# Attention maxima one pair ahead and in bfloat16 parts, a chunk's last sum in the next chunk, squares laid out token by token

## The chip, the cores and the metric

The kernel runs on one core of a Trainium2 chip. The metric is the device time of one execution in microseconds (us). A core has five engines that each work through their own queue: TensorE (PE, matrix products; its weight loads are listed apart as PEld), VectorE (DVE), ScalarE (ACT), GpSimd (POOL), and SyncE (SP), which issues the transfers. Matrix products go into PSUM, which is used here in banks of 512 floats per partition; all else lies in SBUF.

## The reference

Two blocks of a network act on x of 16 sequences, 512 tokens and 256 channels. Each block has an attention part and a feed-forward part; both are normalised, scaled, shifted and gated per sequence.

The attention of block 0 is a recurrence over chunks of 16 tokens, for every sequence and each of 16 heads, with two small weight matrices (4 x 16) that change from chunk to chunk:

```python
def step(carry, xs):
    W_in, W_out = carry
    q_t, k_t, v_t, lr_t = xs
    k_h = softmax(einsum('blhd,bDhd->blhD', k_t, W_in)) * lr_t[..., 1:]
    q_h = softmax(einsum('blhd,bDhd->blhD', q_t, W_in))
    qk = einsum('bqhD,bkhD->bhqk', q_h, k_h) * mask
    o_t = einsum('bqhD,bDhd->bqhd', q_h, W_out) + einsum('bhqk,bkhd->bqhd', qk, v_t)
    W_out = W_out + einsum('bnhD,bnhd->bDhd', k_h, v_t)
    for _ in range(2):
        g_out = -attn(W_in, k_t, v_t)
        g_in = -attn(W_out, v_t, k_t)
        W_in = W_in - lr_in * g_in
        W_out = W_out - lr_out * g_out
    return ((W_in, W_out), o_t)
```

Before it, q and k are divided by their length over the 16 channels of a head, and after it o is normalised over the same channels; both need a sum of squares per token. The feed-forward of block 0 is `gelu(x U1 V1 + b1) U2 V2 + b2`. Block 1 has a softmax attention in which a token sees the 64 last tokens and tokens 0 to 3, and a feed-forward `sigmoid(xr W_r) * (relu(xk W_k)^2 W_v)`.

## The kernel before, in words

**Units.** A unit is 8 sequences (a half) by 64 tokens; there are 16. Each passes through five streams: `prepare` (projections, short convolutions), `chain` (the recurrence), `mlp` (end of block 0's attention, then `low_rank_ffn`), `attend` (`window_attention`), `mix` (`channel_mix`). `timetable` gives every step of a stream a due time; the steps are emitted in that order, two chains (one of each half) always side by side and in the same phase. The framework's scheduler then orders the instructions of each engine by these priorities and its own estimate of when they are ready; on the chip each queue runs in the order so built, and tiles come from rings of buffers.

**The recurrence** (`recur`, one call per chunk, seven steps). Every product of tokens and weights is one elementwise instruction of 1024 numbers per partition and a reduction: `scores` multiplies on DVE (L500) and reduces on DVE (L501); `outer` multiplies on POOL (L507, tiles pd_o, pd_kv, pd_i) and `total` reduces on DVE (L603, tiles do, di). A softmax over tokens is `exp_tokens` (maximum, difference, the exponential on ACT, L515) and `over_tokens` (L520 to L522). In the order of a chunk: scores of k and q; their softmaxes; outer products pd_o (its sum do1, L608) and pd_kv; a running sum over the tokens (L598); scores of v; pd_i twice; scores of k again; pd_o again; and as the last sum of the chunk `do2`, which gives W_out (L624). All product tiles share one ring of five buffers (`prod`), for both halves. Two chunks are a piece of 32 tokens; `load_piece` loads k, v and q and divides by the lengths, `finish_piece` normalises o.

**Squares.** ACT writes the squares in the order of the tile, channel by channel, and `sum_d` (L529) reduces them on DVE over the channels, which lie 32 numbers apart.

**The attention** (`window_attention`). It goes by pairs of sequences r = 0 to 3. For a pair: scores sc, query by key, into four banks (`abank`, a ring of four that st, py, pz and the ph of `low_rank_ffn` share), with the mask added by a bfloat16 product (L828); their maxima over keys on DVE (L850), for all but the first two token blocks also over the four global keys (sg, mg, L862); the maxima turned by PE (L865) and copied by ACT (L867) to mxT; then the same scores key by query, st, from which the maxima are subtracted by products of a selector and mxT; the exponential on ACT (L883); the products with the values and with ones (py, pz); the reciprocal by a logarithm and an exponential (L932, L933); yT on DVE (L937); the projection. The float32 selectors `sel` and `selg` are columns of a constant called parity. The helper `mm` stands for nearly all products there, so they have one line, L831.

**The bias b2** is added in `low_rank_ffn` as a product of a row of ones and the row b2, once for each sequence pair (L724).

Where a function of ACT needs another table, ACT loads it (ACT_TABLE_LOAD); `run` keeps the instructions of a burst of one table together (L204) and loads the usual table again after it (L214).

Of the kernel before, what the change touches and what calls it, by code (L numbers as in the profile page):

```python
# [10 lines left out]
F32 = mybir.dt.float32  # L11
# [20 lines left out]
NS = 4  # L32
F, RANK = 1024, 64
# [34 lines left out]
def parity_scales():  # L68

    ch = np.arange(P)
    even = (ch // D) % 2 == 0
    s = 1.0 / math.sqrt(D)
    group, slot = ch // 32, ch % 32
    sel = -(slot[:, None] == np.arange(NS)[None, :]).astype(np.float32)
    k2, pair, _ = np.unravel_index(np.arange(32), (2, 4, NGLOB))
    selg = np.stack(
        [(group[:, None] == pair) & (slot[:, None] == 2 * k2 + e) for e in range(2)], 1  # L80
    ).astype(np.float32)
    ones_g = np.tile(np.arange(8)[None, :] == (4 * k2 + pair)[:, None], (NR, 1))
    parts = [
        np.stack([even * s, ~even * s, even, ~even], 1),
        group[:, None] == np.arange(4)[None, :],
        sel,
        -selg.reshape(P, -1),
        ones_g,
    ]
    return np.ascontiguousarray(np.concatenate([p.astype(np.float32) for p in parts], 1))  # L90
# [3 lines left out]
def adaln_blocks(ctx: ExitStack, tc: tile.TileContext, a: dict, out: bass.AP):  # L94
# [71 lines left out]
    b2_row = ctile([1, C], "b2_row")  # L166
    nc.sync.dma_start(b2_row, a["V2b"][RANK:])
# [8 lines left out]
    parity, rowgrp, sel = marks[:, :4], marks[:, 4:8], marks[:, 8 : 8 + NS]  # L176
    selg = marks[:, 8 + NS : 72 + NS].rearrange("p (n k) -> p n k", n=2)
    ones_g = marks[:, 72 + NS :]
    ones = ctile([P, 32], "ones")
    nc.vector.memset(ones, 1.0)  # L180
    masks = const.tile([P, 12, P], BF16, tag="masks", name="masks")
# [12 lines left out]
    def log_sigmoid_tail(src, tmp):  # L194
# [3 lines left out]
        nc.scalar.activation(tmp, tmp, AF.Ln, bias=1.0)  # L198

# [26 lines left out]
    with tc.tile_pool(name="mod", bufs=1) as mp:  # L226
        masks_f = mp.tile([P, 12, P], F32, tag="masks_f", name="masks_f")
        nc.sync.dma_start(masks_f, a["masks"].rearrange("p (n k) -> p n k", n=12))
        nc.vector.tensor_copy(masks, masks_f)
        wp = mp.tile([P, 2, C], F32, tag="wp", name="wp")  # L230
# [59 lines left out]
    maxima = [ctile([P, P], f"maxima{n}") for n in range(2)]  # L290
# [237 lines left out]
    def sum_d(t, x, tag):  # L528
        nc.vector.tensor_reduce(t, x.rearrange("p d t -> p t d"), AX.X, add)  # L529

    def load_piece(u, pc):
# [14 lines left out]
        for n in "kq":  # L546
            sq = big(half, f"sq_{n}{tag}")[:, : D * PT].rearrange("p (d t) -> p d t", d=D)
            nc.scalar.activation(sq, s[n], AF.Square)
            ss = small(half, f"ss_{n}{tag}", PT)
            sum_d(ss, sq, tag)  # L550
            inverse_root(ss)
            nc.gpsimd.tensor_tensor(s[n], s[n], over_d(ss), mul)
        return s

    def recur(u, pc, c, s):
# [15 lines left out]
        scores(half, nc.vector, q, w_in, sc[:, :, CH:], f"q{tag}")  # L571
        p_out = exp_tokens(half, sc[:, :, :CH], R, f["mx_k"], f"k{tag}")
# [51 lines left out]
        nc.vector.tensor_tensor(w_out, total(d_out, "do2"), w_outs[:, R:], add)  # L624
# [7 lines left out]
    def finish_piece(u, pc, s):  # L632
# [7 lines left out]
        sum_d(mean, o, tag)  # L640
        nc.scalar.activation(mean, mean, AF.Copy, scale=1.0 / D)
        nc.gpsimd.tensor_tensor(o, o, over_d(mean), sub)
        sq = big(half, f"osq{tag}")[:, : D * PT].rearrange("p (d t) -> p d t", d=D)
        nc.scalar.activation(sq, o, AF.Square)
        var = small(half, f"ov{tag}", PT)
        sum_d(var, sq, tag)
# [39 lines left out]
    def low_rank_ffn(i, x):  # L686
# [27 lines left out]
        yield  # L714
        qT = t2k("b", f"QT{i}")
        nc.scalar.copy(qT, pq)
        for b2 in range(2):
            gt = load_gate("b", 1, b0 + 4 * b2, f"b{i}_{b2}")
            po = bank(f"pv2{i}_{b2}")
            for n in range(2):  # L720
                r = 2 * b2 + n
                dst = po[:, n * C : (n + 1) * C]
                nc.tensor.matmul(dst, lhsT=qT[:, r * P : (r + 1) * P], rhs=w_v2, start=True, stop=False)
                nc.tensor.matmul(dst, lhsT=ones[:1, :1].to_broadcast([1, P]), rhs=b2_row, start=False, stop=True)  # L724
# [3 lines left out]
    def window_attention(i, x):  # L728
# [105 lines left out]
        for b2 in range(NR // 2):  # L834
            gt = load_gate("c", 2, b0 + 4 * b2, f"c{i}_{b2}")
            outs = []
            for n in range(2):
                r = 2 * b2 + n
                tag = f"{i}_{r}"
                q = lambda k2, e: qs[:, k2, 2 * r + e].rearrange("p h t -> p (h t)")  # L840

                sc = [abank(f"sc{tag}_{j}") for j in range(4)]
                for s, k2, e in slots:
                    for j in range(4):
                        rows = slice(32 * j, 32 * (j + 1))
                        mm(sc[j][:, s * P : (s + 1) * P], q(k2, e)[rows], window(r, k2, e)[rows], s == 0)
                mx = maxima[r % 2]
                for j in range(4):
                    add_mask(sc[j], True)
                    nc.vector.tensor_reduce(  # L850
                        mx[:, 32 * j : 32 * j + NS], sc[j].rearrange("p (s k) -> p s k", s=NS), AX.X, ALU.max
                    )
                if far:
                    sg = bank(f"sg{tag}")
                    for s, k2, e in slots:
                        mm(sg[:, 16 * s : 16 * (s + 1)], q(k2, e), kglob[:, b0 + 2 * r + e, 32 * k2 : 32 * k2 + 16], s == 0)
                    mg = work.tile([P, 16], F32, tag="mg", name=f"mg{tag}", bufs=2)
                    nc.vector.tensor_reduce(
                        mg, sg[:, :64].rearrange("p (x g) -> p x g", g=NGLOB), AX.X, ALU.max
                    )  # L860
                    mv = mx.rearrange("p (j x) -> p j x", j=4)[:, :, :NS]
                    nc.vector.tensor_tensor(mv, mv, mg.rearrange("p (s j) -> p j s", s=NS), ALU.max)  # L862
                yield
                pt = bank(f"pmx{tag}")
                nc.tensor.transpose(pt[:, :P], mx, ident)  # L865
                mxT = work.tile([P, P], F32, tag="mxT", name=f"mxT{tag}", bufs=1)
                nc.scalar.copy(mxT, pt[:, :P])  # L867

                st = [abank(f"st{tag}_{j}") for j in range(4)]
                for s, k2, e in slots:  # L870
                    for j in range(4):
                        rows = slice(32 * j, 32 * (j + 1))
                        mm(st[j][:, s * P : (s + 1) * P], window(r, k2, e)[rows], q(k2, e)[rows], s == 0)
                for s, k2, e in slots:
                    for j in range(4):
                        rows = slice(32 * j, 32 * (j + 1))
                        mm(st[j][:, s * P : (s + 1) * P], sel[rows, s : s + 1].to_broadcast([32, P]), mxT[rows])
                yield
                pT = []
                for j in range(4):  # L880
                    add_mask(st[j], False)
                    pT.append(t2k("c", f"pT{tag}_{j}"))
                    nc.scalar.activation(pT[j], st[j], AF.Exp)  # L883
                py, pz = abank(f"py{tag}"), abank(f"pz{tag}")
                if far:

                    rg = slice(32 * r, 32 * (r + 1))
                    tg = bank(f"tg{tag}")
                    for s, k2, e in slots:
                        mm(tg[rg, e * P : (e + 1) * P], kglob[:, b0 + 2 * r + e, 16 * k2 : 16 * k2 + 32], q(k2, e), s == 0)  # L890
                    for e in range(2):
                        mm(tg[rg, e * P : (e + 1) * P], selg[:, e], mxT)
                    pg = work.tile([P, 2 * P], F32, tag="pg", name=f"pg{tag}", bufs=1)
                    nc.scalar.activation(pg[rg], tg[rg, : 2 * P], AF.Exp)
                    for s, k2, e in slots:
                        for j in range(4):
                            cols = slice(k2 * P + 32 * j, k2 * P + 32 * (j + 1))
                            mm(
                                py[32 * j : 32 * (j + 1), s * P : (s + 1) * P],
                                vglob[half][rg, e, cols],  # L900
                                pg[rg, e * P : (e + 1) * P],
                                s == 0,
                            )
                    for k2 in range(2):
                        for j in range(4):
                            n = 4 * k2 + j
                            mm(
                                pz[32 * j : 32 * (j + 1), k2 * 2 * P : (k2 + 1) * 2 * P],
                                ones_g[rg, n : n + 1].to_broadcast([32, 32]),
                                pg[rg],  # L910
                                k2 == 0,
                            )
                for s, k2, e in slots:
                    for j in range(4):
# [3 lines left out]
                            values[:, r, e, cols],  # L918
                            pT[j][:, s * P : (s + 1) * P],
                            s == 0 and not far,  # L920
                        )
                for s, k2, e in slots:
                    for j in range(4):
                        mm(
                            pz[32 * j : 32 * (j + 1), s * P : (s + 1) * P],
                            ones,
                            pT[j][:, s * P : (s + 1) * P],
                            s == 0 and not far,
                        )
                yield  # L930
# [206 lines left out]
```

## Time and profile before

| | us |
|---|---|
| runs without a profile: median of 3 (lowest, highest) | 3312.57 (3311.25, 3323.61) |
| the profiled execution: its own time | 3313.35 |
| its span, first to last instruction | 3311.6 |
| table loads on ACT, all lines: one | 1.28 |
| one outer product on POOL (L507) | 2.35 |
| one product or reduction of the recurrence on DVE (L500, L501, L603) | 1.21 to 1.22 |
| one reduction to maxima (L850) | 0.68 |

The mean granted clock of TensorE was 0.815 of full speed. Names of tiles are given without the numbers of unit, pair and chunk, so that `do` covers both do1 and do2 and one row stands for all units. A row of groups gives line, engine, operation, what is written and read with partitions and elements, the count; then the busy time in us and the mean of one in ns; then how long the engine had been idle before them and what ended most of that. An fp32 product shows as two records. A row of waits gives who waited for whom, the us in total, how often, and the longest. A row of stages gives the stretch and its length, the busy time of each engine, then the granted clock, the share of the transfer engines and GB/s.

### The profile page before, as it was taken

How to read it: one execution, taken by the hardware profiler on the slowest of the kernel's cores; microseconds unless marked ns; L12 is line 12 of the kernel's file. 1: busy time of each engine (PE TensorE's matmuls, PEld its weight loads, DVE VectorE, ACT ScalarE, POOL GpSimd, SP SyncE). 2: the span in 40 equal slices, each digit the busy share in tenths (PEclk: the TensorE clock that was granted, in tenths of full speed). 3: DMA queues.
4: the chain of work that ended last, by engine and by line, in shares of the span. 5: the costliest groups of instructions: out<-in, count | busy, mean ns of one | idle time of the engine just before them, and what ended most of it. 6: DMA issues, size and time to landing. Idle time of an engine off the chain costs nothing.

```text
span 3311.6 us, 48552 instructions
## 1 busy us (share of the span) xinstructions
PE 2415.2 (73%) x18000; PEld 1495.9 (45%) x18000; DVE 2404.3 (73%) x4510; ACT 1714.0 (52%) x3731; POOL 1613.8 (49%) x1255
## 2 busy tenths in 40 slices
PE   3550155868687787878788787877777787889996
PEld 2110124444344454444545445454445555556674
DVE  1678787778878888888787888878787887864211
ACT  1662254556465645565665546565565544454542
POOL 0335555455556555545556554645546565644101
PEclk9765576879788787888888788888888787878988
DMA  5330113131314122230313123140413221122000
GB/s 148 78 67 15 45 31 70 30 72 43 77 33 97 37 68 62 51 79 27 94 29 97 39 57 74 37 94 21 100 23 82 48 58 46 46 49 58 17 27 26
DMA packets 439215, 186.54 MB, mean 56 GB/s; under 512 B 323841, under 2 KB 412994, under 8 KB 438978
## 3 DMA queue, kind: packets, MB, share of 16 engines
q1 hardware_dynamic: 438978, 183.44, 23.0%
q8 instruction: 141, 2.31, 0.3%
q14 instruction: 96, 0.79, 0.1%
HBM read 116.66 MB, written 66.72 MB: 55 GB/s over the span
## 4 chain that ended last, share of the span: by engine, by line
DVE 36%; POOL 23%; PE 19%; ACT 10%; issue 9%; DMA 2%; SPq 1%; POOLq 0%; ACTq 0%; DVEq 0%
POOL pd_i L507 6%; POOL pd_o L507 6%; DVE pd_kv L598 4%; DVE sc_v L500 3%; DVE sv L501 3%; POOL pd_kv L507 3%; DVE pp L433 3%; DVE maxima L850 2%; DVE di L603 2%; PE ph L704 2%; PE st L831 2%; DVE scs L501 2%; DVE do L603 2%; DVE sc_k L500 2%; PE pp L415 2%
## 5 line engine op out<-in xcount | busy, mean ns | idle before, releaser
L507 POOL TENSOR_TENSOR pd_o<-e_k,dt_v 128x1024 f32<-128x1024 f32 x128 | 299.3, 2348 | 331.1 <-DVE e_k L522 330.9
L507 POOL TENSOR_TENSOR pd_i<-e_v,dt_k 128x1024 f32<-128x1024 f32 x128 | 296.5, 2350 | 73.4 <-DVE e_v L522 73.4
L831 PE MATMUL st<-qs,keys 32*128 32x128 f32 x2048 | 244.1, 384 | 118.4 <-DVE maxima L850 116.9
L831 PEld LDWEIGHTS st<-qs,keys 32*128 32x128 f32 x2048 | 206.3, 265 | 164.3 <-DVE maxima L850 138.9
L603 DVE TENSOR_REDUCE do<-pd_o 128x64 f32<-128x1024 f32 x128 | 155.7, 1216 | 158.0 <-POOL pd_o L507 157.8
L628 POOL TENSOR_TENSOR pd_kv<-hid,pd_kv 128x1024 f32<-128x1024 f32 x64 | 150.5, 2352 | 151.9 <-DVE fw L599 148.8
L603 DVE TENSOR_REDUCE di<-pd_i 128x64 f32<-128x1024 f32 x128 | 155.6, 1215 | 94.6 <-POOL pd_i L507 94.6
L676 PE MATMUL pwo<-w_WoT,oT 128*128 128x256 f32 x256 | 103.4, 567 | 148.1 <-POOL oT L669 148.1
L831 PE MATMUL sc<-keys,qs 32*128 32x128 f32 x2048 | 169.1, 307 | 58.1 <-DVE yT L937 33.9
L850 DVE TENSOR_REDUCE maxima<-sc 128x4 f32<-128x512 f32 x256 | 166.6, 680 | 35.7 <-PE sc L828 35.7
L831 PEld LDWEIGHTS sc<-keys,qs 32*128 32x128 f32 x2048 | 136.7, 199 | 114.5 <-issue 41.9
L598 DVE TENSOR_TENSOR_SCAN pd_kv<-within,pd_kv 128x1024 f32<-128x1024 bf16 x64 | 174.4, 2725 | 0.4
L500 DVE TENSOR_TENSOR sc_k<-tok,fw 128x1024 f32<-128x1024 f32 x128 | 155.8, 1217 | 17.5 <-ACT tok L565 15.2
L507 POOL TENSOR_TENSOR pd_kv<-hid,dt_v 128x1024 f32<-128x1024 f32 x64 | 150.4, 2350 | 33.1 <-DVE hid L590 28.9
L883 ACT ACTIVATE pT<-st 128x512 f32<-128x512 f32 x256 | 133.5, 620 | 35.5 <-PE st L828 35.5
L500 DVE TENSOR_TENSOR sc_v<-tok,fw 128x1024 f32<-128x1024 f32 x128 | 150.9, 1212 | 0.9
L501 DVE TENSOR_REDUCE sv<-sc_v 128x64 f32<-128x1024 f32 x128 | 151.0, 1208 | 0.0
L997 POOL TENSOR_TENSOR ka<-ka 128x512 f32<-128x512 f32 x32 | 32.8, 1039 | 238.1 <-ACT ka L996 238.1
L947 PE MATMUL pproj<-w_proj,yT 128*128 128x256 f32 x512 | 131.5, 402 | 23.4 <-DVE yT L937 19.6
L676 PEld LDWEIGHTS pwo<-w_WoT,oT 128*128 128x128 f32 x256 | 70.2, 291 | 172.4 <-POOL oT L669 157.0
L204 ACT ACT_TABLE_LOAD x104 | 133.4, 1283 | 25.8 <-PE ph L704 16.4
L428 ACT COPY xp<-pp 128x512 f32<-128x512 f32 x96 | 56.7, 590 | 170.9 <-PE pp L415 159.3
(237 smaller groups left out, 6823.5 us busy)
## 6 DMA issues: line engine op xcount, KB each, us to landing
values<-values SPq DMA_DIRECT2D x56, 256.0 KB
gate_a<-gates SPq DMA_DIRECT2D x64, 128.0 KB
xa<-in_x_dram SPq DMA_DIRECT2D x32, 256.0 KB
x<-in_x_dram SPq DMA_DIRECT2D x32, 256.0 KB
gate_c<-gates SPq DMA_DIRECT2D x64, 128.0 KB
gate_d<-gates SPq DMA_DIRECT2D x64, 128.0 KB
q<-y SPq DMA_DIRECT2D x64, 128.0 KB
dt_q<-q SPq DMA_DIRECT2D x32, 256.0 KB
```

What stands on the lines that cost most here:

```text
L204: ins = nc.scalar.activation(*args[0], **args[1])
L500: engine.tensor_tensor(pr, tok.unsqueeze(1).to_broadcast(every), w.unsqueeze(2).to_broadcast(every), mul)
L501: nc.vector.tensor_reduce(dst, pr, AX.X, add)
L507: engine.tensor_tensor(pr, hid.unsqueeze(2).to_broadcast(every), tok.unsqueeze(1).to_broadcast(every), mul)
L598: nc.vector.tensor_tensor_scan(flat, within, flat, 0.0, mul, add)
L603: nc.vector.tensor_reduce(t, pr, AX.X, add)
L628: nc.gpsimd.tensor_tensor(po, qh.unsqueeze(2).to_broadcast([P, R, D, CH]), upto, mul)
L676: nc.tensor.matmul(po[:, n * C : (n + 1) * C], lhsT=pair(oT, k, 2 * b2 + n), rhs=w_o[:, k, :], start=k == 0, stop=k == 1,)
L831: nc.tensor.matmul(dst, lhsT=lhsT, rhs=rhs, start=start, stop=False, skip_group_check=True)
L850: nc.vector.tensor_reduce(mx[:, 32 * j : 32 * j + NS], sc[j].rearrange("p (s k) -> p s k", s=NS), AX.X, ALU.max)
L883: nc.scalar.activation(pT[j], st[j], AF.Exp)
L947: nc.tensor.matmul(po[:, n * C : (n + 1) * C], lhsT=yT[:, k2, par].rearrange("p e t -> p (e t)"), rhs=w_proj[:, k2, par, :], start=k2 == 0 ...
```

## The change

It has five parts.

1. The work on a pair is split into `find_maxima` (scores, maxima) and `weigh` (all the rest). The first pair's maxima are found ahead of the loop, and then those of pair r + 1 are issued before pair r is weighed.
2. The maxima are kept as three bfloat16 numbers that add up to the float32 one, in 12 of each 32 columns of the tile `maxima`, made by five small instructions on POOL (`in_parts`). The tile, the identity that turns it, mxT and the selectors are bfloat16; a selector now has a one for each of the three parts.
3. b2 is three bfloat16 rows (`bias2`), made at the start by DVE and moved to three partitions by three small transfers; one product over a whole bank adds it for both pairs, ahead of the products with V2.
4. The last sum of a chunk and its addition to W_out (`do2`) are kept as a function and called in the next chunk of the same half, after the scores of k and q. After the last chunk of a half they are left out, since nothing reads W_out then.
5. ACT writes the squares token by token, so that the 16 that are added lie side by side; `squares` takes the place of `sum_d`.

```diff
-    sel = -(slot[:, None] == np.arange(NS)[None, :]).astype(np.float32)
+    part = slot // NS < NPART
+    sel = -((slot[:, None] % NS == np.arange(NS)[None, :]) & part[:, None]).astype(np.float32)
...
+    sel_bf = const.tile([P, NS + 64], BF16, tag="sel_bf", name="sel_bf")
+    nc.vector.tensor_copy(sel_bf, marks[:, 8 : 72 + NS])
...
+    def in_parts(engine, parts, x, rest):
+
+        for n in range(NPART):
+            engine.tensor_copy(parts[n], x)
+            if n < NPART - 1:
+                engine.tensor_tensor(rest, x, parts[n], sub)
+                x = rest
...
+        in_parts(nc.vector, [b2_parts[:, n] for n in range(NPART)], b2_row, b2_row)
+        for n in range(NPART):
+            nc.sync.dma_start(bias2[n : n + 1], b2_parts[:, n])
...
-    maxima = [ctile([P, P], f"maxima{n}") for n in range(2)]
+    maxima = [const.tile([P, P], BF16, tag=f"maxima{n}", name=f"maxima{n}") for n in range(2)]
...
-    def sum_d(t, x, tag):
-        nc.vector.tensor_reduce(t, x.rearrange("p d t -> p t d"), AX.X, add)
+    def squares(half, x, name):
+
+        sq = big(half, name)[:, : D * PT].rearrange("p (t d) -> p t d", d=D)
+        nc.scalar.activation(sq.rearrange("p t d -> p d t"), x, AF.Square)
+        return sq
...
-            sq = big(half, f"sq_{n}{tag}")[:, : D * PT].rearrange("p (d t) -> p d t", d=D)
-            nc.scalar.activation(sq, s[n], AF.Square)
+            sq = squares(half, s[n], f"sq_{n}{tag}")
             ss = small(half, f"ss_{n}{tag}", PT)
-            sum_d(ss, sq, tag)
+            nc.vector.tensor_reduce(ss, sq, AX.X, add)
...
         scores(half, nc.vector, q, w_in, sc[:, :, CH:], f"q{tag}")
+        late[half]()
         p_out = exp_tokens(half, sc[:, :, :CH], R, f["mx_k"], f"k{tag}")
...
-        nc.vector.tensor_tensor(w_out, total(d_out, "do2"), w_outs[:, R:], add)
+        late[half] = lambda: nc.vector.tensor_tensor(w_out, total(d_out, "do2"), w_outs[:, R:], add)
...
+            nc.tensor.matmul(
+                po, lhsT=ones_bf, rhs=b2_rows, start=True, stop=False, skip_group_check=True
+            )
...
-                nc.tensor.matmul(dst, lhsT=ones[:1, :1].to_broadcast([1, P]), rhs=b2_row, start=False, stop=True)
...
+        def find_maxima(r):
...
+            mx = work.tile([P, 4, NS], F32, tag="mx", name=f"mx{tag}", bufs=2)
+            for j in range(4):
+                add_mask(sc[j], True)
+                nc.vector.tensor_reduce(
+                    mx[:, j], sc[j].rearrange("p (s k) -> p s k", s=NS), AX.X, ALU.max
+                )
...
+            parts = maxima[r % 2].rearrange("p (j x) -> p j x", j=4)
+            rest = work.tile([P, 4, NS], F32, tag="rest", name=f"rest{tag}", bufs=2)
+            in_parts(nc.gpsimd, [parts[:, :, NS * n : NS * (n + 1)] for n in range(NPART)], mx, rest)
+
+        def weigh(r, outs):
...
-                nc.tensor.transpose(pt[:, :P], mx, ident)
-                mxT = work.tile([P, P], F32, tag="mxT", name=f"mxT{tag}", bufs=1)
+            nc.tensor.matmul(pt[:, :P], lhsT=maxima[r % 2], rhs=ident_bf, start=True, stop=True)
+            mxT = work.tile([P, P], BF16, tag="mxT", name=f"mxT{tag}", bufs=1)
...
+        find_maxima(0)
+        yield
+        for b2 in range(NR // 2):
+            gt = load_gate("c", 2, b0 + 4 * b2, f"c{i}_{b2}")
+            outs = []
+            for r in (2 * b2, 2 * b2 + 1):
+                if r + 1 < NR:
+                    find_maxima(r + 1)
+                    yield
+                yield from weigh(r, outs)
+                yield
```

The number of steps of `attend` in the timetable is the same as before.

## The prediction

> **What bounds the kernel now.** I read the page first (busy shares and slices), then the busy times of three stages, then those of one unit, then who waits for whom, last the groups.
>
> ```profile
> span 3311.6 us, 48552 instructions
> PE 2415.2 (73%) x18000; PEld 1495.9 (45%) x18000; DVE 2404.3 (73%) x4510; ACT 1714.0 (52%) x3731; POOL 1613.8 (49%) x1255
> PE   3550155868687787878788787877777787889996
> DVE  1678787778878888888787888878787887864211
> POOL 0335555455556555545556554645546565644101
> ```
>
> There are three stages: a start with little for PE, a long middle in which PE and VectorE (DVE) are about equally busy, and an end with PE alone. The sums by stage (PE, weight loads, DVE, ACT, POOL):
>
> ```profile
> 0.00:522.00 522.00, 201.51 (x476) 90.44 (x476) 352.21 (x643) 213.74 (x453) 217.27 (x197) 0.71 0.29 66
> 522.00:3026.00 2504.00, 1966.92 (x15033) 1232.40 (x15033) 1990.41 (x3722) 1380.66 (x3026) 1351.97 (x1013) 0.83 0.24 58
> 3026.00:3312.00 286.00, 246.74 (x2492) 173.06 (x2491) 61.66 (x145) 119.54 (x254) 44.52 (x47) 0.87 0.11 29
> ...
> sum 188.02, PE 149.68 PEld 93.41 DVE 151.30 ACT 106.33 POOL 100.22; mean PE 74.84 PEld 46.71 DVE 75.65 ACT 53.17 POOL 50.11
> ```
>
> The last line is one unit in the middle (1712.56 to 1900.58): 188 us, DVE 151, PE 150. No engine is full; the time is the busy time of DVE plus the waits that two coupled queues impose. What DVE waits for in the middle:
>
> ```profile
> DVE do L603 <- POOL pd_o L507: 132.5, 85, 3.6
> DVE di L603 <- POOL pd_i L507: 78.7, 50, 3.1
> DVE yT L937 <- ACT rs L933: 29.6, 14, 3.5
> DVE up_a L361 <- PE pwo L676: 19.8, 13, 2.1
> DVE up_c L361 <- PE pproj L947: 14.8, 11, 2.5
> ```
>
> And PE over the whole run, then the groups that the change touches or is priced by:
>
> ```profile
> PE st L831 <- DVE maxima L850: 116.9, 36, 8.0
> ...
> L831 PE MATMUL st<-mxT,c_parity 32*128 32x128 f32 x2048 | 113.7, 358 | 4.8 <-ACT mxT L867 4.8
> L724 PE MATMUL pv<-b_row,ones 1*128 1x256 f32 x128 | 46.6, 445 | 0.0
> L529 DVE TENSOR_REDUCE ss_k<-sq_k 128x32 f32<-128x512 f32 x32 | 32.3, 1010 | 2.0 <-ACT sq_k L548 2.0
> L501 DVE TENSOR_REDUCE sv<-sc_v 128x64 f32<-128x1024 f32 x128 | 151.0, 1208 | 0.0
> L520 DVE TENSOR_REDUCE fw<-e_v 128x8 f32<-128x128 f32 x64 | 18.4, 288 | 3.4 <-ACT e_v L515 1.7
> L430 POOL COPY tails<-xp 128x24 f32<-128x24 f32 x84 | 20.1, 240 | 65.0 <-ACT xp L428 62.9 <-ACT om L641 1.9
> ```
>
> **What the Trainium skill says.** "PSUM — Partial Sum Buffer", section "Engine vs sequencer instructions": the queues of ScalarE, VectorE and GpSimdE are strictly first in, first out. The trace agrees: at 1733.62 a pd_o product on POOL starts only after two ka squares, the first of which waited 15.29 us for ACT. "SBUF — State Buffer", section "Door 1: The DMA port swizzle": SBUF lines are 16 bytes, and an access that crosses into a new line pays. The trace agrees for reads: L529 reads 512 elements with a stride in 1010 ns, L501 1024 adjacent ones in 1208. "FP8 and Floating Point Precision", section "TensorE Precision Notes": true FP32 takes four passes. The trace has four bf16 mask products of 512 columns (L828) in 0.97 us, 0.24 each, and an fp32 one (L704) in two records, 1.1 us. "ScalarE: Activation LUTs", section "What ACT_TABLE_LOAD costs": 1283 ns and a drain of about 1380. The trace shows the 1283, and the activation after it 20 ns later; I use 1.28 us.
>
> **The change part by part.**
>
> *bf16 selectors, maxima and bias (PE).* Per pair of sequences, 16 selector products into st are 32 fp32 records, 113.7 / 64 = 1.78 us; undisturbed, 32 such records take 1.07 us, 33 ns each[...]. In bf16 there are 16 records, about 0.53 us; I take 0.9 saved (0.5 to 1.2). The two selectors of tg and the turned maxima halve: 0.5 together. So 1.4 us a pair, 64 pairs: 90. The bias falls from 128 records, 46.6 us, to 32 bf16 products at 0.26: 38 saved. PE loses about 128 us, 8 a unit. In the end stage PE is the bound: 324 records there read mxT or the selectors, 36 a pair, so 9 pairs x 1.4 = 12.6, and one unit's bias 2.4: **-15**. In the middle it counts only where DVE waits on PE's side: yT, up_a, up_c, together 64 us. With 8 of PE's 150 us gone and mxT ready early I take a third: **-20** (0 to -64).
>
> *Maxima one pair ahead.* This looks as if it removed PE's 117 us wait for the maxima. It does not: four banks hold either scores sc or weights st, so st of a pair now waits until DVE has read sc of the next pair. The chain maxima, turn, copy, selectors goes off PE's path, the bank wait stays. Beyond what is counted above I take 0.
>
> *Parts on POOL.* Five small instructions per pair, 320 in all. Copies of 24 elements take 240 ns; at 0.22 each that is 1.1 us a pair, 70 us, in a POOL that is idle half the time. They stand in line, though: in the order built from the changed program the fourth pair's five are right ahead of pd_o, the third's ahead of pd_i. Two exposed groups a unit for 13 units are 29; I take **+10** (0 to 70).
>
> *The chunk's last sum (do2).* Of the 132.5 us above, sorting the L603 reductions by the addition after them (L608 or L624), 58.6 of the run's waits belong to the second sum. In the new order sc_k, sc_q and their reductions of the next chunk, 4 x 1.2 us, come first, longer than the product of 2.35, so this wait goes. Late next is do1, whose 75 us stay. The pd_o buffer is held longer: the ring has five, at most two are held so, three remain. Where a piece ends the reduction already comes first in the new order. I take 60%: **-35** (0 to -58).
>
> *Squares token by token.* 96 reductions (k, q, o in 32 pieces) become contiguous: between 288 ns for 128 elements and 1208 for 1024, 512 give 0.68 against 1.01 to 1.05. 96 x 0.34 = 33 us of DVE; at DVE's 79% of the middle **-25**. ACT now writes with a stride. No row shows that; the strided read of tok (256 elements, 643 ns against about 420 by the rows of 128 and 512) bounds it: 0 to +0.45 us each, 0 to 43 us on an engine busy 55%. Seven more table loads in the new order (ACT puts e_k inside the gelu burst) are 9 us. For both **+5** (0 to 50).
>
> *Start.* Three small loads of the bias parts wait in SP's queue for DVE, with w_init and the second wm behind them; that wm waits until 38 us anyway for its buffer. 0 (to +4).
>
> Sum: -15 -20 +10 -35 -25 +5 = -80. The profiled execution took 3313.35 (span 3311.6), within 1 us of the median 3312.57: **3233 us**.
>
> **The rivals.** *Waits fill up again.* A wait removed from one of two coupled queues returns at the next: only busy time counts, -25 and -15: 3273. For it: DVE and PE are equally full, do1 and di remain. Against: do2's cover is DVE's own work.
>
> *More falls away.* ka's squares stood ahead of pd_o1 and cost do1 3.6 and 1.4 us a unit; in the new order they stand among the pd_i products. That would be 5 x 13 = 65 more, and the 64 us of PE-side waits wholly 44 more: 3124. Against: ka can then hold up pd_i.
>
> *Slower: the chain stands behind PE.* In the new order the second chunk's e_k is normalised on DVE (L541) only after the fourth pair's maxima and the second up_b. PE's work from the first ph to that up_b's product, by the durations of before (8 ph 8.8, 8 pQ 8, pr 3.7, pproj 3.5, scores and masks 2.9, plr and pp 3.5, pkv 1.9, bias and pv 2.2, small ones 3.5), is 38 us, and it starts some 4.6 before e_k2. With 1.1 on POOL and 2.4 on DVE, pd_o1 starts 37 us after e_k2; before it was 1703.33 to 1733.62, 30.3. Seven us a unit, 12 units, +84, against -40 of sure gains: 3357. It decides from 3.3 us a unit. Against: much of DVE's later work is done in that time.
>
> **How the numbers follow.** Forecast 0.43 (own range 3190 to 3275), refilled waits 0.22, more falls away 0.17, slower 0.18. About 0.5%, 17 us, is what a measurement of this kernel can tell from no change. Faster: 0.43 + 0.21 + 0.17 less a little; same 0.04; slower 0.16. The range takes in the third rival's better half and the slower one's beginning, 3130 to 3335.
>
> **What would show it.** Right: L624's sums without waits; ss, ov near 0.68 us; selector products under 0.6 us a pair; the stage after the last chain some 15 us shorter; the unit at 183 us. Wrong: DVE idle before e_k or the last maxima with PE as releaser; POOL's product waiting on the parts; a unit at or over 188.

## The result, and the profile after

The changed kernel took 3296.14 us (median of 5 runs, 3289.18 to 3303.97) beside 3317.76 for the kernel before in the same session: a ratio of 0.9937 (95% interval 0.9913 to 0.9961). It is 0.6% faster, some 21 us, a quarter of the 80 that the prediction gave. Its profiled execution took 3303.97, 3302.2 of them in the span; the mean granted clock of PE was 0.780 (before 0.815). This execution is the slowest of the five, and the other four had 0.785 to 0.789, so the profile shows less than half of the gain and a clock somewhat lower than usual.

The page after (busy time, share and instructions by engine, then two engines in 40 slices):

```profile
span 3302.2 us, 46348 instructions
PE 2424.1 (73%) x16784; PEld 1461.5 (44%) x16784; DVE 2396.2 (73%) x4513; ACT 1762.1 (53%) x3738; POOL 1669.3 (51%) x1575
...
PE   3541255777787878788887878788797878878886
DVE  1678787868887787788778877877878877774221
```

PE has 1216 records fewer and is busy 9 us *longer*. The same three stages after, columns as before:

```profile
0.00:522.00 522.00, 205.24 (x506) 94.86 (x506) 359.34 (x660) 221.88 (x464) 224.92 (x209) 0.67 0.28 66
522.00:3026.00 2504.00, 1993.54 (x13999) 1215.08 (x14000) 1979.59 (x3719) 1420.53 (x3029) 1392.88 (x1281) 0.80 0.24 58
3026.00:3302.00 276.00, 225.30 (x2285) 151.57 (x2282) 57.27 (x136) 119.71 (x248) 51.46 (x86) 0.85 0.10 28
```

In the middle DVE idles 2504 - 1980 = 524 us; before it was 514. The unit there is hardly shorter (before 188.02):

```profile
sum 187.50, PE 153.01 PEld 92.08 DVE 151.91 ACT 110.27 POOL 102.80; mean PE 76.51 PEld 46.04 DVE 75.95 ACT 55.13 POOL 51.40
```

What DVE waits for in the middle after:

```profile
DVE do L628 <- POOL pd_o L526: 87.4, 54, 4.1
DVE di L628 <- POOL pd_i L526: 68.2, 48, 3.2
DVE yT L972 <- ACT rs L968: 33.9, 16, 4.5
DVE ss_q L571 <- ACT sq_q L550: 25.1, 7, 6.7
DVE mix L1022 <- ACT mix L1021: 22.4, 7, 8.3
DVE ov L670 <- ACT osq L550: 20.2, 19, 3.1
DVE sc_q L519 <- ACT tok L589: 19.6, 24, 3.1
DVE pd_kv L620 <- POOL pd_kv L526: 18.8, 11, 2.5
DVE up_c L380 <- PE pproj L994: 18.6, 15, 9.5
```

The waits for do and di fell from 211.2 to 155.6 us, as meant. Waits for ACT grew by as much in the same stretch: ov from 0.3 to 20.2, qs from 0.5 to 17.7, mix from 10.1 to 22.4, fw (for e_k) from 5.2 to 17.2. What was taken from one producer stands at another.

Now PE, in the groups of after:

```profile
L865 PE MATMUL st<-mxT,sel_bf 32*128 32x128 bf16 x1024 | 55.1, 247 | 29.6 <-ACT mxT L902 29.5
L745 PE MATMUL pv<-bias,ones_bf 3*128 3x512 bf16 x32 | 12.3, 383 | 0.0
L865 PE MATMUL py<-pT,values 128*32 128x128 f32 x2048 | 130.4, 374 | 26.8 <-ACT pT L918 26.3
L865 PE MATMUL py<-pg,vglob 32*32 32x128 f32 x1536 | 71.8, 342 | 99.1 <-ACT pg L929 99.1
L865 PE MATMUL pz<-pg,c_parity 32*32 32x256 f32 x768 | 86.8, 534 | 0.0
```

and two of these groups before:

```profile
L831 PE MATMUL py<-pT,values 128*32 128x128 f32 x2048 | 96.4, 289 | 21.0 <-ACT pT L883 20.6
L831 PE MATMUL pz<-pg,c_parity 32*32 32x256 f32 x768 | 57.2, 378 | 0.0
```

The products that were changed cost what was forecast: st's selectors 113.7 to 55.1, the bias 46.6 to 12.3, with the two small ones 119 us less (forecast 128). But products that nobody touched became longer: py from pT by 34, pz from pg by 30, the other two of that kind (pz from pT, py from pg) by 50, together 113. Why is seen in the granted clock. Four stretches of after's middle, columns as in the stages, the granted clock third from the end, and two more that show how long the clock stayed down:

```profile
1739.00:1743.00 4.00, 3.25 (x48) 2.06 (x46) 2.48 (x7) 3.07 (x6) 3.92 (x6) 1.00 0.21 69
1743.00:1748.50 5.50, 0.00 (x0) 0.00 (x0) 5.01 (x13) 4.47 (x7) 5.42 (x7) 0.77 0.54 145
1748.50:1752.00 3.50, 3.45 (x48) 2.13 (x48) 2.31 (x4) 1.09 (x2) 2.04 (x2) 0.50 0.80 154
1752.00:1756.00 4.00, 4.00 (x70) 3.26 (x67) 3.93 (x3) 0.00 (x0) 1.44 (x1) 0.50 0.83 131
...
1748.50:1756.20 7.70, 7.65 (x115) 5.58 (x116) 6.40 (x7) 1.09 (x2) 3.64 (x3) 0.50 0.80 138
1756.20:1759.61 3.41, 0.85 (x8) 0.50 (x6) 3.41 (x4) 0.00 (x0) 3.33 (x2) 1.00 0.00 0
```

PE idles for 5.5 us, its clock drops from 1.00 to 0.50, and it stays there for the work that follows. PE's timeline at that place (start, length, in brackets the wait) in after:

```profile
1748.55 1.93 PE L865 MATMUL py<-pg,vglob 32*32 32x128 f32 x32 [5.59 <-ACT pg L929]
```

and in before:

```profile
1773.26 1.07 PE L831 MATMUL py<-pg,vglob 32*32 32x128 f32 x32 [1.08 <-ACT pg L894]
```

The same 32 records take 1.93 instead of 1.07 us. The Trainium skill, "TensorE: Matmul & The Clock Gate", section "Part 1: The HAM clock gate (the "warmup" mystery)", states this: half rate after an idle window of some 3.4 us, full rate after a busy one. The trace agrees on the fall: PE fell idle at 1742.96 and the clock fell at 1745.96, 3.0 us later. The rise took longer here: PE was busy for 7.65 of 7.70 us before the clock rose at 1756.20. In both traces the record of the clock has no value but 1.0 and 0.5, so a mean of 0.780 is 44% of the span at half rate and 0.815 is 37%: about 230 us more in this execution. Laid over PE's busy time, half rate covers 807 us of it before and 1030 after. Half of the difference, 112 us, is about what the four groups gained (113), an estimate from the two traces. The prediction has no term for it.

PE's waits over the whole run after, to be held against 116.9 us of st for the maxima before:

```profile
PE py L865 <- ACT pg L929: 99.1, 40, 5.7
PE st L865 <- DVE mx L881: 47.8, 16, 5.8
PE sc L865 <- DVE mx L881: 43.4, 22, 6.8
PE st L865 <- ACT rs L967: 36.1, 6, 6.3
```

The bank wait stays, spread over st and sc: with all releasers of their banks, st and sc waited 118.4 + 58.1 us before and 107.2 + 63.0 after. And py's wait for ACT's exponential over the global keys, 17.8 before, became 99.1.

### The profile page after: what moved, and what is told of

It reads as the page before. It is cut to its first block, busy times and chain, and to the rows that moved or that the text cites. A ratio compares the mean times of both kernels' runs of the same rounds, so it can differ in the third digit from the quotient of the medians.

```text
span 3302.2 us, 46348 instructions
## 1 busy us (share of the span) xinstructions
PE 2424.1 (73%) x16784; PEld 1461.5 (44%) x16784; DVE 2396.2 (73%) x4513; ACT 1762.1 (53%) x3738; POOL 1669.3 (51%) x1575
## 4 chain that ended last, share of the span: by engine, by line
DVE 32%; PE 28%; POOL 18%; ACT 11%; issue 7%; DMA 3%; SPq 1%; POOLq 0%; DVEq 0%; ACTq 0%
POOL pd_o L526 4%; POOL pd_i L526 4%; DVE pd_kv L623 4%; DVE pp L452 3%; DVE sc_v L519 3%; PE ph L728 3%; PE py L865 3%; PE st L865 2%; PE pz L865 2%; DVE sv L520 2%; PE pproj L994 2%; POOL pd_kv L526 2%; DVE mx L881 2%; DVE do L628 2%; PE pka L1031 2%
## 5 line engine op out<-in xcount | busy, mean ns | idle before, releaser
L865 PE MATMUL st<-qs,keys 32*128 32x128 f32 x2048 | 234.3, 351 | 107.2 <-DVE mx L881 47.8
L865 PEld LDWEIGHTS st<-qs,keys 32*128 32x128 f32 x2048 | 199.5, 240 | 163.0 <-DVE mx L881 61.5
L881 DVE TENSOR_REDUCE mx<-sc 128x4 f32<-128x512 f32 x256 | 168.4, 679 | 19.0 <-PE sc L862 19.0
L865 PE MATMUL py<-pT,values 128*32 128x128 f32 x2048 | 130.4, 374 | 26.8 <-ACT pT L918 26.3
L972 DVE TENSOR_TENSOR yT<-py,rs 128x256 f32<-128x256 f32 x128 | 51.5, 415 | 133.8 <-ACT rs L968 133.7
L865 PE MATMUL py<-pg,vglob 32*32 32x128 f32 x1536 | 71.8, 342 | 99.1 <-ACT pg L929 99.1
```

The lines of the kernel that those rows point to most:

```text
L865: nc.tensor.matmul(dst, lhsT=lhsT, rhs=rhs, start=start, stop=False, skip_group_check=True)
L881: nc.vector.tensor_reduce(mx[:, j], sc[j].rearrange("p (s k) -> p s k", s=NS), AX.X, ALU.max)
```

## The experiments

Ratios are to the kernel before, measured beside each; times multiplied from a ratio use 3317 us. "Order held" means: each engine's instructions stand in the order of a given kernel, written in as neighbours without a wait:

```python
for first, then in zip(names, names[1:]):
    tc.add_manual_dep(here[then], first,
        mybir.DependencyInfo(mybir.DependencyClass.NoSync, mybir.DependencyReason.DATA), reason="order held")
```

Otherwise the scheduler makes the order anew.

### One part alone

**1. Squares alone.**

```diff
-            sq = big(half, f"sq_{n}{tag}")[:, : D * PT].rearrange("p (d t) -> p d t", d=D)
-            nc.scalar.activation(sq, s[n], AF.Square)
+            sq = squares(half, s[n], f"sq_{n}{tag}")
```

> The kernel before with the squares written token by token and nothing else. Prediction: 96 reductions fall from 1.01 to 0.68 us (-33 us of VectorE), ScalarE pays little, the time falls by about 20 us, to 3298. Rival: ScalarE's strided squares cost 0.45 us each (43 us, as in the trace after) and are waited for by VectorE, which gives the 33 us back: 3310 to 3325, with some 30 us more waits on sq_q, osq and hid.

3320.33 us, ratio 1.0006 (0.9998 to 1.0015): nothing. The order was the same as before, so the sizes can be read off: 0.68 us for DVE's reductions and 1.08 for ACT's squares, as in the groups of after:

```profile
L571 DVE TENSOR_REDUCE ss_k<-sq_k 128x32 f32<-128x512 f32 x32 | 21.8, 681 | 8.2 <-ACT sq_k L550 5.4 <-ACT ov L196 2.4
...
L550 ACT ACTIVATE sq_k<-dt_k 128x512 f32<-128x512 f32 x32 | 34.3, 1073 | 1.3 <-DMA dt_k<-k 1.3
```

against ACT's squares before:

```profile
L548 ACT ACTIVATE sq_k<-dt_k 128x512 f32<-128x512 f32 x32 | 19.9, 623 | 3.8 <-DMA dt_k<-k 3.8
```

DVE gained 0.33 us a piece, as forecast; ACT lost 0.45, the upper bound. DVE's waits grew by 42 us, 10 each at yT and up_c, and not mainly at the squares, where the rival had put them. At the yT of 1811.98, shown under the ninth experiment, DVE waited 4.54 us for ACT instead of 3.50.

**2. The late sum alone.**

```diff
-        nc.vector.tensor_tensor(w_out, total(d_out, "do2"), w_outs[:, R:], add)
+        late[half] = lambda: nc.vector.tensor_tensor(w_out, total(d_out, "do2"), w_outs[:, R:], add)
```

> The kernel before with the chunk's last sum put into the next chunk and nothing else. Prediction: the 58.6 us of waits of do2 go and 60% of it is kept: 3283. Rival: the waits of do fall by 57 us but return elsewhere (do1, di, yT, PE's side): 3305 to 3318.

3327.63, ratio 1.0036 (1.0023 to 1.0049): slower by 12 us, although the waits for do fell by 79. ov, mix, the maxima and ss_q together waited 101 more. The order was made anew here.

**3. bfloat16 parts alone** (against the changed kernel: without 1, 2 and the pair ahead; each pair's maxima right before its weights).

```diff
-                if r + 1 < NR:
-                    find_maxima(r + 1)
-                    yield
+                find_maxima(r)
+                yield
                 yield from weigh(r, outs)
```

> The kernel before with the maxima, selectors and bias in bfloat16 parts (five small instructions of GpSimd for each pair) but with every pair's maxima found just before it is weighed, as before. Theory A (ScalarE's table loads between the four exponentials of a pair leave PE idle, and the clock falls to half; this needs the maxima one pair ahead too): no table load stands between them here, the granted clock stays at 0.81 or above, PE's busy time falls by 80 us or more, the time by 20 to 60 us, to 3260 to 3300. Theory B (any work taken off PE opens gaps that halve its clock): the clock falls to 0.79 or below, PE's busy time stays within 40 us of 2415, and the time stays above 3305.

**4. One pair ahead alone** (against the changed kernel: without 1, 2 and everything in bf16, the bias too).

```diff
-            parts = maxima[r % 2].rearrange("p (j x) -> p j x", j=4)
-            in_parts(nc.gpsimd, [parts[:, :, NS * n : NS * (n + 1)] for n in range(NPART)], mx, rest)
...
-            mxT = work.tile([P, P], BF16, tag="mxT", name=f"mxT{tag}", bufs=1)
+            mxT = work.tile([P, P], F32, tag="mxT", name=f"mxT{tag}", bufs=1)
```

> The kernel before with the maxima found one pair ahead, all in float32, and nothing else. Prediction: nothing beyond the bank wait that stays: 3313, within 15 us. Theory A: two table loads stand between exponentials here (22 in the changed kernel), so the clock stays near 0.81. Rival: the order one pair ahead alone makes PE wait for pg and brings the clock to 0.79 or below and the time to 3320 or more.

Both were slower: 3371.66, ratio 1.0167 (1.0152 to 1.0181), and 3371.83, ratio 1.0172 (1.0157 to 1.0187). In the third the turning of the maxima shows what the parts do when they are not a pair ahead:

```profile
L899 PE MATMUL pmx<-ident_bf,maxima 128*128 128x128 bf16 x64 | 17.4, 272 | 189.0 <-POOL maxima L208 113.8 <-ACT y L217 75.3
```

PE waits 113.8 us for the five instructions on POOL. In the fourth, py waited 150.0 us for pg. But two kernels, each slower by 55 us, whose parts together are faster: that is no sum of parts, and the order became the suspect.

### One part undone

**5, 6, 7.** The changed kernel without the squares; without the late sum; with neither (bf16 parts and one pair ahead alone). The edits are those of 1 and 2, backwards.

> The changed kernel with ScalarE's squares written as before the change; the order on PE, VectorE and GpSimd is that of the changed kernel. The prediction's step (VectorE's 33 us count, ScalarE pays little) asks for some 20 us more: 3316. What the run with the squares alone says (the two cancel): 3290 to 3302. If ScalarE's 43 us are waited for in full and VectorE's 33 us are cover: 3280 or less.

> The changed kernel with the last sum of a chunk where it was before the change. The prediction's step asks for 35 us more: 3331. If the sum in the next chunk costs here what it cost alone (+11 us): 3285. The waits of do2, 57 us, come back in either case.

> The kernel before with the bfloat16 parts and the maxima one pair ahead together, without the squares and the late sum. Each alone made the kernel 55 us slower. If the two need each other (the parts on GpSimd are hidden only one pair ahead, and the order one pair ahead pays only when the selectors are cheap): 3280 to 3310. If their costs add: 3400 or more. With 22 table loads between exponentials in its order, the clock should be 0.79 or below, and PE wait for pg some 100 us.

| | us | ratio (interval) |
|---|---|---|
| 5 squares undone | 3293.49 | 0.9921 (0.9908 to 0.9935) |
| 6 late sum undone | 3282.89 | 0.9891 (0.9876 to 0.9906) |
| 7 both undone | 3284.03 | 0.9896 (0.9880 to 0.9913) |

The whole gain is in the two parts of the attention: with them alone (7) the kernel is 14 us faster than with all five (0.0041, give or take 0.003). The queues of 5 stand in after's order and those of 7 in that of 6, so these two pairs show the squares alone: nothing, in either order. Between after and 6 and between 5 and 7 the order was made anew. The 15 and 8 us in these two pairs are those of another order as much as of the late sum.

### The waits for pg, and the clock

**8. The four exponentials of a pair together.** In after's order 22 table loads stand between them, before none.

```diff
+                with tc.high_priority():
                     nc.scalar.activation(pT[j], st[j], AF.Exp)
```

> The changed kernel with a higher priority for the four exponentials of a pair, so that two table loads instead of 22 stand between them. Theory A (ScalarE's late exponentials leave PE idle, its clock falls to half and its products take twice as long): the wait of py for pg falls from 99 us to 50 or less, the granted clock rises to 0.80 or more, PE's busy time falls below 2370, the time to 3240 to 3280. Rival (VectorE's chain bounds the kernel, PE's slower products lie beside it): PE's figures may change as said, the time stays within 15 us of 3296.

3322.02, ratio 1.0015 (1.0005 to 1.0025). The wait for pg became shorter:

```profile
PE py L865 <- ACT pg L930: 64.7, 35, 4.5
```

The edit did what it should (2 table loads between them), but two thirds of the wait stayed, the clock stayed at 0.78 and PE's busy time did not fall (2432.7). So most of this wait does not hang on the table loads. The kernel lost 26 us, which decides nothing, since the order had been made anew again.

### The order held

**9. The late sum, order held** (before's order; only do2 moved).

> The kernel before with the late sum only, as in the second experiment, but every engine's queue holds the order of the kernel before; the sum and its addition alone are moved. The prediction's 60% of the waits of do2: 3283. If the +11 us of the second experiment came from the order that the scheduler made anew: 3305 or less. If the waits of do2 come back by themselves at the next waits (ScalarE's squares, mix, the product of the first sum): 3312 to 3330.

3344.86, ratio 1.0093 (1.0076 to 1.0110): 31 us slower, about 3 us a unit (191.1 against 187.8, the mean of four units). Nothing but do2 stands elsewhere, so the stretch can be laid side by side. DVE's timeline at the end of a piece, before:

```profile
1798.35 1.22 DVE L603 TENSOR_REDUCE do<-pd_o 128x64 f32<-128x1024 f32 x1 [1.64 <-POOL pd_o L507]
...
1811.98 0.76 DVE L937 TENSOR_TENSOR yT<-py,rs 128x256 f32<-128x256 f32 x2 [3.50 <-ACT rs L933]
...
1828.61 1.21 DVE L501 TENSOR_REDUCE scs<-sc_q 128x64 f32<-128x1024 f32 x1
1829.73 0.22 DVE L512 TENSOR_REDUCE fw<-scs 128x4 f32<-128x64 f32 x1
```

and in the ninth:

```profile
1814.49 0.76 DVE L443 SCALAR_TENSOR_TENSOR pp<-xp,w_ck,pp 128x512 f32<-128x512 f32 x1 [3.58 <-ACT pp L441]
...
1823.69 0.76 DVE L951 TENSOR_TENSOR yT<-py,rs 128x256 f32<-128x256 f32 x2 [3.50 <-ACT rs L947]
...
1840.36 1.21 DVE L511 TENSOR_REDUCE scs<-sc_q 128x64 f32<-128x1024 f32 x1
1841.48 1.21 DVE L619 TENSOR_REDUCE do<-pd_o 128x64 f32<-128x1024 f32 x1
1842.73 0.23 DVE L640 TENSOR_TENSOR fw<-do,fw 128x64 f32<-128x64 f32 x1
1842.99 0.23 DVE L522 TENSOR_REDUCE fw<-scs 128x4 f32<-128x64 f32 x1
```

The 1.64 us of waiting and do2's own time are gone from the first place. DVE came early to pp and waited 3.58 for ACT, and then 3.50 at yT as before: from the last scaling of e_k (1796.43 before, 1808.35 here) to yT it took 15.55 us before and 15.34 here. From yT to the softmax it was 17.75 before and 19.30 here: do2 stands behind the last wait of this stretch, so its 1.44 us of work count in full. The chunk of the other half, 7 us later, loses another 1.51 at its own softmax (1837.11 before, 1851.86 here): 3 us a unit. At the chunk inside a piece gains and losses cancel: DVE was 11.92 us later than in the kernel before where it starts and 11.93 where it ends. Over the whole run do's waits fell by 72 us, while those for ACT grew by 21 at pp, 23 at yT and 13 at ov.

This is the price of one place, right behind the reduction of sc_q, in one order. In the changed kernel the scheduler put only 2 of the 62 late sums there, so the 31 us are not what the late sum costs in it.

**10. bf16 parts, order held** (before's order, the parts on POOL right after the maxima).

> The kernel before with the bfloat16 parts and bias only, as in the third experiment, but every engine's queue holds the order of the kernel before, and the five parts of a pair stand on GpSimd behind what was issued when their maxima were. The prediction's terms (-15 -20 +10): 3288. If the +55 us of the third experiment came from the order made anew: 3310 or less. If the parts wait on GpSimd behind its long products and PE waits for them (189 us of PE's waits before the turn of the maxima in the third experiment): 3340 or more.

3348.95, ratio 1.0097 (1.0080 to 1.0114): 32 us slower, though PE was busy 90 less. The maxima's parts stand in POOL's queue behind long products:

```profile
L899 PE MATMUL pmx<-ident_bf,maxima 128*128 128x128 bf16 x64 | 17.0, 265 | 81.6 <-POOL maxima L208 56.5 <-ACT y L217 20.0 <-DVE up_a L380 5.1
```

**11. PE kept busy.** Kernel 7, order held, with 24 useless bf16 products ahead of py in two of four pairs of each unit with far keys.

```diff
+            if r in (1, 2):
+                for n in range(24):
+                    nc.tensor.matmul(tg[:, 2 * P :], lhsT=ident_bf, rhs=masks[:, :2],
+                                     start=n == 0, stop=n == 23, skip_group_check=True)
```

> The kernel of bfloat16 parts and maxima ahead (3284), order held, with 24 useless bfloat16 products of 256 columns into an unused half of tg's bank ahead of py, in the second and third pair of each unit with far keys, where PE waits 1.8 to 6.5 us for pg. Theory A (the half clock after these waits costs time): the clock rises to 0.80 or more, the products of py and pz that follow take about 0.27 and 0.37 us for most pairs, the time falls by 10 to 40 us. Rival (PE's slower products lie beside VectorE's chain): the clock rises, the time stays within 8 us of 3284 or rises.

3274.20, ratio 0.9869 (0.9855 to 0.9884) against 0.9896 for the seventh: added work took off some 9 us, give or take 7; the two intervals just overlap. The clock rose from 0.787 to 0.803, and pz from pg took 465 ns instead of 515. So the half clock may cost something of this size, and not the whole of what is missing.

**12. A nudge.** The kernel before, with the due time of `mix` 0.05 units earlier, nothing else.

```diff
-[(8, u + 4.1, u + 4.7)]
+[(8, u + 4.05, u + 4.65)]
```

> The kernel before with nothing changed but the due time of the channel mix, 0.05 of a unit earlier: the same instructions, in an order that the scheduler makes anew. If the order made anew is worth little: 3317 within 8 us. If a large part of the 55 us of the single parts is the order: 20 us or more away from 3317, to either side.

3357.22, ratio 1.0127 (1.0112 to 1.0142): 41 us lost by an edit that changes no instruction. Differences of this size between kernels whose order was made anew say nothing about their parts; this goes for 2 to 4, 6, 7 and 8, and for the changed kernel itself.

**13. One part for the maxima, order held** (before's order; the reduction on DVE writes one bfloat16 number, the two smaller parts are left out, POOL has nothing).

```diff
-    part = slot // NS < NPART
+    part = slot // NS < 1
...
-            mx = work.tile([P, 4, NS], F32, tag="mx", name=f"mx{tag}", bufs=2)
+            mx = maxima[r % 2]
...
-            in_parts(nc.gpsimd, [parts[:, :, NS * n : NS * (n + 1)] for n in range(NPART)], mx, rest)
```

> The kernel before with bfloat16 selectors, maxima and bias, its order held, and a single bfloat16 part that VectorE's maximum writes itself: the two smaller parts are left out, so what is subtracted ahead of the exponential is the maximum rounded to bfloat16, in numerator and denominator alike. No work on GpSimd. The prediction's terms (-15 at the end, -20 in the middle): 3282. If the 128 us taken off PE count only at the end: 3300. If PE's gaps bring its clock down and eat it: 3310 or more, with a clock of 0.79 or less.

3313.97, ratio 0.9989 (0.9982 to 0.9996): PE was busy 85 us less, and 3.5 came out.

```profile
522.00:3026.00 2504.00, 1889.12 (x13969) 1155.58 (x13969) 1986.86 (x3724) 1378.76 (x3022) 1351.20 (x1012) 0.81 0.24 57
```

PE's 78 us in the middle became idle time, and its clock fell from 0.83 to 0.81. By stages: the start is 6.5 us later (DVE waits 19.2 us for the transfer of the selectors before it copies them), the middle 1 shorter, the stretch after the last scan 4.7 shorter. The wait of st for the maxima is as long as ever, 115.0 us:

```profile
PE st L864 <- DVE maxima L880: 115.0, 36, 6.9
```

### What the order is worth

**14. The same with the seventh's order held, one pair ahead.** Edit: 13's, in kernel 7.

> The kernel of bfloat16 parts and maxima ahead (3284), its order held, with the single part as in the run before: GpSimd's 320 small instructions are left out. If one pair ahead hides them, as the prediction has it (+10): 3274. If they still hold up GpSimd's long products: 3265 or less. If they cost nothing: 3284.

3264.08, ratio 0.9841 (0.9827 to 0.9855). Against the seventh, in the same order, the parts on POOL cost 18 us.

**15, 16. Nudges.** Kernel 7 with the nudge of 12; before with a nudge of 0.05 the other way.

> The kernel of bfloat16 parts and maxima ahead (3284) with the due time of the channel mix 0.05 of a unit earlier, order made anew; the kernel before went from 3317 to 3357 by the same nudge. If the gain of parts and maxima ahead is their own, this is some 33 us below the nudged kernel before: 3324. If the orders are chance: anywhere from 3270 to 3370.

> The kernel before with nothing changed but the due time of the channel mix, 0.05 of a unit later. If the kernel before stands at a good point of its orders: slower here too, 3330 or more. If the nudge to the other side cost 41 us for a reason of its own: 3317 within 10 us, or faster.

3357.70, ratio 1.0126 (1.0110 to 1.0142), the same as the nudged kernel before; and 3321.64, ratio 1.0017 (1.0010 to 1.0024). With other due times the gain of the two parts is not there. The nudge the other way cost only 6 us, so an order made anew is not always a bad one.

**17. float32, the fourteenth's order held** (maxima, identity, mxT and selectors in float32; the bias in bf16).

```diff
-    maxima = [const.tile([P, P], BF16, tag=f"maxima{n}", name=f"maxima{n}") for n in range(2)]
+    maxima = [ctile([P, P], f"maxima{n}") for n in range(2)]
```

> The kernel of the single part and maxima ahead (3264) in its own order, with the maxima and selectors in float32 again (the bias stays in bfloat16). If the order alone carries the gain over the kernel before: 3264 to 3280. If the cheaper selectors carry it within this order (PE's waits end on the chain from the maxima to the values there): 3300 or more; PE's busy time is some 85 us more than with the single part.

3271.05, ratio 0.9854 (0.9837 to 0.9870). The order does it without the short type in the maxima: 48 of the fourteenth's 53 us. Against the fourth, which differs by the bias and by the order, the ratio is 0.9854 where it was 1.0172: over 100 us. One pair ahead is thus not enough for the gain. Whether it is needed, or an order as good exists without it, no run shows.

**18. The fourteenth with PE kept busy** (11's edit).

> The kernel of the single part and maxima ahead (3264), order held, with the 24 useless products ahead of py in the second and third pair. If what they gave before (10 us) adds to the single part: 3254. If the single part has taken the same wait away: 3260 to 3270. The two smaller parts of the maxima are left out, as before.

3262.41, ratio 0.9831 (0.9816 to 0.9846), the fastest of all, though not told apart from the fourteenth. It leaves out the smaller parts of the maxima and has the useless products. The clock rose here too, from 0.791 to 0.804, and pz from pg fell from 503 to 424 ns, without a measurable gain: the 9 us of the eleventh did not come again.

## Why the prediction was wrong

**The step that failed most: do2, -35.** "In the new order sc_k, sc_q and their reductions of the next chunk ... come first, longer than the product of 2.35, so this wait goes", and "I take 60%". The wait went: do's waits in the whole middle fell by 45 us, those of the second sum from 57.1 to 10.7 in the changed kernel, and do1's 75 stayed, as forecast. The time did not go. In the order held, DVE is bound by ACT (pp, rs) ahead of yT, so what is saved there is waited for there; and the sum itself moved behind the last wait. There it cost 31 us. What it costs in the changed kernel is not separated from the order. "Late next is do1" named the next wait for the same producer, where the next wait on the same engine was asked for.

**bf16 on PE, -15 and -20.** The 128 us of PE were right (119). Their worth was not: -3.5 in before's order. In the end stage, after the last scan, they gave 4.7 in the thirteenth; in the changed kernel that stretch is 10 us longer (327.4 against 317.0), while the chain ends 20 earlier. In the middle, the third of DVE's waits on PE's side that should have gone stayed: yT, up_a and up_c waited 64 us before and 57 in the thirteenth, yT for ACT's rs as before (29.6 and 29.5), and st for DVE's maxima. The clock fell with the added idle time (0.83 to 0.81 in the thirteenth), and in the changed kernel PE's busy time came back whole, as longer products.

**One pair ahead, 0 beyond the rest.** The argument, that the bank wait stays, was right: st and sc wait 170 us for their banks where they waited 177. But the part changes the order, and orders here differ by 100 us: +57 in the fourth, -48 in the seventeenth. This is where the measured gain comes from, and the sum had no term for it. That the order came out well is luck: it was not forecast, and a nudge of 0.05 took the gain away.

**Parts on POOL, +10 (0 to 70).** 231 ns each were taken as 0.22; the cost is 18 us one pair ahead, and 36 where PE needs them at once (10 against 13).

**Squares, -25 and +5.** DVE's 33 us were right, ACT's 43 at the bound of "0 to 43". Net 0 in three orders; in the first experiment the gain went into waits, the largest for ACT at yT and for PE at up_c.

**Start, 0.** The first scan came 0.1 us earlier in after; in the thirteenth's order 6.5 later.

Of the signs named ahead, ss and ov at 0.68 us were right. do2's sums do wait less. The selector products took 55.1 / 64 = 0.86 us a pair and not under 0.6; in the pairs that ran at the full clock throughout it was 0.41 (median of 33), so the sign failed by the half clock. The unit is 187.5, not 183. Of the rivals the first, waits that fill up again, is the nearest in kind, and the time lies beyond it; the slower one, 7 us more a unit, did not come.

The account from the runs, as the way from the kernel before over 17, 14 and 7 to the changed kernel: order with one pair ahead, with the bias in bf16, -48; bf16 maxima there -4 (not resolved); parts on POOL +18; late sum and squares, with an order made anew, +14. These are differences of successive ratios, so that they add up to the measured -21 (within rounding) proves nothing. The second and third are the price of an edit in a held order; the first and the last are in part or wholly the price of an order.

Open: which feature of an order makes it 100 us better or worse. What the wait for pg is worth (8) is not shown; the clock (11 and 18) is worth some 9 us or nothing; the rest was not found.

## What to carry to other kernels

Before pricing a wait that goes, look at the next wait on the same engine, and at the place where moved work lands: in the ninth experiment time saved ahead of a wait for another engine was worth nothing, and work put behind the last wait cost its full length. Where a scheduler orders the queues anew, hold the order to measure an edit, or first measure what a neutral nudge does. Work taken from an engine that waits on others can become idle time, as 78 us of PE's did in the thirteenth, and here PE's clock fell with it.

## What the runs showed of the hardware

- PE's granted clock fell from 1.00 to 0.50 within a wait of 5.5 us, and the next 32 records took 1.93 instead of 1.07 us. 24 useless products before such places raised the mean clock in two kernels (0.787 to 0.803, 0.791 to 0.804); one became 9 us faster, the other not measurably.
- An activation that writes 512 float32 numbers per partition with a stride took 1073 ns, adjacent 623. A DVE reduction that reads 512 with a stride took 1010, adjacent 681.
- Small instructions on POOL (16 elements per partition) took 231 ns each:

```profile
L208 POOL CAST maxima<-rest 128x16 bf16<-128x16 f32 x128 | 29.5, 231 | 7.6
```
